# A two-dimensional scan block on one core: the order of small matmuls, copies and stores between the stages of a pair

## The chip, the core and the metric

The kernel runs on one core of one Trainium2 chip, as one program. The metric is the device time of the whole program in microseconds. The engines that matter are TensorE (PE, matmuls; PEld, its weight loads), VectorE (DVE), ScalarE (ACT), GpSimd (POOL) and SyncE (SP), which issues the DMAs. All data are fp32. An fp32 matmul shows in the trace as two records, called passes here.

## What is computed

The input x has the shape (4, 128, 96, 96). It is group-normalised, read as four sequences of 9216 positions (row by row, column by column, and both backwards), and each sequence runs through the same block. The reference, cut to what matters:

```python
t = _grouped1x1(x, in_proj_w, in_proj_b, G)          # 4 groups of 32 channels -> 512
u, gate = t[:, :HID], t[:, HID:]                     # HID = 256
u = depthwise_conv5(silu(u), dw_w)
s = ssm_in_w @ u                                     # 32 channels
a = clip(DMIN + (DMAX - DMIN) * sigmoid(ssm_delta_w @ u + ssm_delta_b), 1e-4, 0.9999)
bb, cc = tanh(ssm_b_w @ u + ssm_b_b), tanh(ssm_c_w @ u + ssm_c_b)
hst = scan(h = a * h + bb * s)                       # along the sequence
u = u + ssm_out_w @ (cc * hst + ssm_d * s)
y = out_proj_w @ (mix(u * sigmoid(gate)) + mix_b) + out_proj_b
```

The four outputs are put back in image order, concatenated, multiplied by fuse_w (128 x 512) and added to x. Before the loop the kernel folds mix, out_proj and fuse of each direction into one weight `w_fin`, called W below.

## The kernel before

**Tiling.** An image is done in two phases, V (columns) and H (rows). A phase has NS = 6 steps, a step 4 x 384 positions. The positions of a step are dealt to R = 4 residues p, so that an instruction works on 384 columns. A unit is one residue of one direction. A *pair* is the units of both directions (s = 0 and 1), and `pair(t)` (L747) runs 192 times; t counts pairs, i = 2t is the pair's first unit, k = t % 4 its residue, and bi = i - 12 is the unit that is finished in this pair (LAG = 6 pairs behind). There is a prologue before the first pair and a `tail` for the last six.

**What a pair does,** in the order in which it is written out by hand (there is a manual schedule, so every engine takes its instructions in this order):

- `front` (L413): only in the steps of the first half of a phase. It computes silu(in_proj) of a later step, 32 small matmul records in 32x32 tiles, and four Silu on ScalarE (L476). The second half of a phase goes backwards over the same data, so it loads what `keep_silu` (L449) stored to DRAM. `load_front` (L249) loads x_in.
- `taps` (L599): the conv of channels 128 to 255, one tap on ScalarE (L609), four on VectorE (L611), summed in PSUM banks 0 and 1, the last one written to u.
- `conv` (L576): the conv of channels 0 to 127 on TensorE, matmuls with 128 rows and the weight `band`; `conv_less` (L585) adds the taps that need only 64 rows, with the weight `less`, and copies both banks to u.
- `accumulate` (L700): W for a unit finished earlier, eight matmuls with 32 columns each, a copy `ys` on ScalarE (L712, L714), and an addition to the image in SBUF on GpSimd (L728).
- `under` (L498): ScalarE seeds the PSUM banks of ssm_out with u (L501), s = 1 in banks 2 and 3, s = 0 in banks 0 and 1.
- `gates_and_out` (L536): four matmuls for the gate (L487), 32 rows and 128 columns, and four for ssm_out (L493) of the same form; then `sigmoids` (L503), four Tanh on ScalarE (L509). A gate is needed in both halves of a phase. In the second half it comes from DRAM (`load_kept`, L522), or from the buffer, and the pair is *old*.
- `gating` (L552): VectorE multiplies u by the gate (L563).
- `proj` (L623): the four projections of u, in PSUM banks 4 and 5 (`PROJ`), first all of channels 128 to 255 (j = 1), then of 0 to 127 (j = 0); Tanh, copy and Tanh on ScalarE (L639 to L641); the decay (L644) and a product (L647) on GpSimd.
- `scale_s` (L662): ScalarE multiplies s by ssm_d (L664). `scan` (L670) is on VectorE, `outputs` (L685) on GpSimd.

**Kinds of pairs,** from the seventh pair on. From `fresh` (L245) and `mirror` (L259), with t % 24: 8 to 17 have gates and no front (gates alone, 80 of the 192); 20 to 23 and 0 to 5 have old gates and a front; 18 and 19 old gates and no front; 6 and 7 gates and a front. Where there is no front, `plan` (L124) gives banks 7 and 6 to the conv and banks 4 and 5 to W; with a front it is the other way round. In the pairs without a front the order on TensorE is: band, W, W, less, gates and ssm_out, projections. There the banks of the gates are banks 4 and 5 (after both W) and 7 and 6 (after the copies of u).

**Queues.** [...] `later` holds pieces of the next image's statistics, done in pairs with k > 1 (`stats_piece`, L782), where VectorE also reads chunks of the next image (L397).

Of the kernel before, what the change touches and what calls it, by code (L numbers as in the profile page):

```python
# [55 lines left out]
R = 4  # L56
# [10 lines left out]
def conv_preact_kernel(  # L67
# [53 lines left out]
    FRONT = (7, 6, 2, 3)  # L121
    GATE = {True: (6, 4, 5, 7), False: (4, 5, 7, 6)}

# [293 lines left out]
    def front_parts(i, banks):  # L417

        step, g = divmod(i, R)
        if step * UB >= NU:  # L420
            return
        st = step % NS
        if st == NS // 2:
            sils[step] = sils[step - 1]
            load_silu(step + 1, (g,))
        elif st == NS - 1 and g < 2:
            load_silu(step, (2 * g, 2 * g + 1))
        elif g == 0 and fresh(step):
            sils[step] = wk.tile([P, 2, 2, 4, N + 1], F32, tag="sil", name=f"sil_{step}")
        if fresh(step):  # L430
            yield from compute_front(step, g, banks)
        sil = sils[step]

        if st == 0:
            engine = nc.gpsimd if step else nc.vector
            for s in range(2):
                engine.memset(sil[64 * s : 64 * s + 64, s, 0, g, 0:1], 0.0)
            if g < 2:
                engine.memset(sil[:, :, 1, g, 0:1], 0.0)

        for s in range(2):
            load_front(step + 1, s, slice(64 * s + 32, 64 * s + 64), slice(g, g + 1))
        if g == R - 1:
            for s in range(2):
                load_front(step + 1, s, slice(64 * s, 64 * s + 32), slice(0, R))
        if step:
            keep_silu(step, g)

    def keep_silu(step, g):  # L449
        st = step % NS  # L450
        if st < NS // 2 - 1:
            nc.sync.dma_start(kept_sil[step // NS % 2][st][g], sils[step][:, :, :, g, :])

# [48 lines left out]

    def sigmoids(bi, banks):  # L503
        bn = stats[units[bi]["b"]][1]
        n = bi // 2
        gv = gates[n % 2]
        for s in range(2):
            for j in range(2):
                nc.scalar.activation(  # L509
                    gv[:, s, j, :],  # L510
                    bank(banks[2 * s + j])[:, :N],
                    AF.Tanh,
                    bias=bn[:, 2 + j : 3 + j],
                    scale=0.5,
                )
# [20 lines left out]
    def gates_and_out(bi, with_front):  # L536
# [4 lines left out]
        if with_front:  # L541
            gate(bi, 1, 0, to[2])
        out_of(bi, 1, 0)
        out_of(bi, 0, 0)
        out_of(bi, 0, 1)
        out_of(bi, 1, 1)
        if not with_front:
            gate(bi, 1, 0, to[2])
        gate(bi, 1, 1, to[3])
        sigmoids(bi, to)  # L550
# [25 lines left out]
    def conv(i, banks):  # L576

        step, p = units[i]["step"], units[i]["p"]
        sil, k = blocks(step), less_of(p)
        for s in range(2):  # L580
            for g in range(4):
                mm(bank(banks[s]), g, band[:, s, p, g, :], columns(step, sil[s][:, g, :], 1 - k),
                   True, False)

    def conv_less(i, banks, copies=(nc.scalar.copy, nc.scalar.copy)):  # L585
        step, p = units[i]["step"], units[i]["p"]
        sil, k = blocks(step), less_of(p)
        for g in range(4):
            for s in range(2):
                r = less_rows(s, p)  # L590
                mm(bank(banks[s]), g, less[r, p, g, :], columns(step, sil[s][r, g, :], k),
                   False, True)
        for s, copy in enumerate(copies):
            copy(us[i][:, s, 0, :], bank(banks[s])[:, :N])  # L594

# [26 lines left out]

    def proj(i, banks):  # L623

# [6 lines left out]

        for j in (1, 0):
            for bk, cols in zip(banks, ((qb, qb, qa, qa), (qs, qs, qc, qc))):
                for c in range(4):
                    mm(bank(bk), c, w_proj[:, j, cols[c]], us[i][:, c % 2, j, :], j == 1, j == 0)
        pa, pb = (bank(bk)[:, :N] for bk in banks)
# [98 lines left out]

    later = []

# [9 lines left out]
    def pair(t):  # L747
# [10 lines left out]
        if back:  # L758
            front(t + R, FRONT)
        if seed and not with_front:  # L760
            under(bi, 1)
# [30 lines left out]
        if waiting and not late:  # L792
            accumulate(waiting.pop(0), w[0])()
        if seed and not with_front:
            under(bi, 0)
        if ahead:
            accumulate(waiting.pop(0), w[1])()
            free[0] = w[0]
            stats_piece()

            other = nc.vector.tensor_copy if k > 1 and not old else nc.scalar.copy
            conv_less(i, banks, (nc.scalar.copy, other))
        if old:
            for s in range(2):
                for j in range(2):
# [11 lines left out]
        if back:  # L817
            load_kept(bi // 2 + 2)
            if waiting:
# [3 lines left out]
            first_tap(i + 2)  # L823
            scale_s(i - 2)
        if t == NU // 2 - 1:
            for s in range(2):
                under(bi + 2, s)
        proj(i, PROJ)
        if not back and t > 0:
            scale_s(i - 2)  # L830
# [5 lines left out]
        if t == NU // 2 - 3:  # L836
            load_last()
        if t < R:
            keep_silu(0, t)

# [137 lines left out]
```

## Time and profile before

| | |
|---|---|
| time, median of 3 runs | 1869.76 us (1868.79 to 1873.79) |
| profiled run, span | 1866.4 us, granted TensorE clock 0.990 |
| TensorE busy | 1827.3 us (98%) |
| VectorE busy | 1561.9 us (84%) |
| ScalarE busy | 1542.6 us (83%) |
| GpSimd busy | 1567.0 us (84%) |
| DMA | 321.21 MB, mean 172 GB/s |

Of the profile four things are read. The busy shares say which engine has no time left. The chain of waits follows the last instruction back to whatever released it. The groups give the mean duration of each form of instruction and the idle time before it. The timeline shows the instructions in order, merged where one engine repeats the same one, with the idle time before each and what ended it. The start of the projections, which every pair has once, is a good mark: from one to the next is the length of a pair. A busy TensorE is not TensorE at its peak: passes that overlap show as longer records, so the distance between the starts of passes is what counts.

### The profile page before, as it was taken

Reading aid. Unit: us, or ns where it says so; the run is one execution under the profiler, and the core shown is the slowest. Engines: PE = TensorE matmul, PEld = TensorE weight load, DVE = VectorE, ACT = ScalarE, POOL = GpSimd, SP = SyncE. Lnnn points to the kernel's source line nnn. Section 1 sums busy time; section 2 is a strip of 40 time slices with the busy share of each in tenths; the row PEclk is TensorE's granted clock in tenths of the full one; section 3 lists DMA queues with packets and bytes.
Section 4 is the critical chain, followed back from the end, with each engine's and each line's share of the span. In section 5 each row is a group of like instructions: output and inputs, shape, how many; then the busy total and the mean of one; then the engine's idle time right before and its main releaser. Section 6 shows DMA issues by size and latency. Waiting matters only on the chain.

```text
span 1866.4 us, 57669 instructions
## 1 busy us (share of the span) xinstructions
PE 1827.3 (98%) x24024; PEld 691.4 (37%) x24024; DVE 1561.9 (84%) x1573; ACT 1542.6 (83%) x2841; POOL 1567.0 (84%) x1615
## 2 busy tenths in 40 slices
PE   6899999999999999999999999999999999999998
PEld 3234333443334433344333433334333443334432
DVE  4698878888888988888889898888887888878886
ACT  4688888888888888888888888888888888888875
POOL 6388988888879899888887989888888889997886
PEclk7999999999999999999999999999999999999999
DMA  5564463433875557243596556433467634535424
GB/s 194 162 197 145 146 207 118 168 141 126 274 244 202 169 155 215 86 158 131 186 301 217 167 162 207 152 130 126 139 224 234 231 113 156 191 118 175 145 102 171
DMA packets 147828, 321.21 MB, mean 172 GB/s; under 512 B 14192, under 2 KB 115696, under 8 KB 147568
## 3 DMA queue, kind: packets, MB, share of 16 engines
q1 hardware_dynamic: 147136, 316.56, 51.5%
q8 instruction: 190, 3.11, 0.7%
q10 hardware_dynamic: 432, 0.96, 0.1%
q14 instruction: 70, 0.57, 0.1%
HBM read 185.21 MB, written 132.25 MB: 170 GB/s over the span
## 4 chain that ended last, share of the span: by engine, by line
PE 87%; ACT 4%; POOL 3%; DVE 2%; DMA 1%; issue 1%; SPq 0%; POOLq 0%; DVEq 0%; ACTq 0%
PE psum L133 73%; PE psum L487 7%; PE psum L493 7%; ACT sil L476 1%; DMA xs<-in_xr 1%; ACT psum L609 1%; DVE u L563 1%; DVE psum L611 1%; POOL acc L728 1%; POOL t L644 1%; ACT u L594 0%; POOL t L647 0%; DMA x_in<-in_xs 0%; POOL t L687 0%; POOL t L688 0%
## 5 line engine op out<-in xcount | busy, mean ns | idle before, releaser
L611 DVE SCALAR_TENSOR_TENSOR psum<-sil,small,psum 128x768 f32<-128x768 f32 x576 | 589.0, 1023 | 39.1 <-ACT psum L609 13.5
L133 PE MATMUL psum<-u,w_fin 128*32 128x384 f32 x6144 | 535.6, 488 | 0.0
L133 PE MATMUL psum<-u,main 128*32 128x384 f32 x6144 | 534.9, 489 | 0.3 <-DVE u L611 0.3
L563 DVE SCALAR_TENSOR_TENSOR u<-gate,psum 128x768 f32<-128x768 f32 x376 | 349.9, 952 | 165.9 <-ACT u L594 91.6
L728 POOL TENSOR_TENSOR acc<-ys,acc 128x384 f32<-128x384 f32 x376 | 412.7, 1118 | 21.6 <-ACT ys L714 4.3
L687 POOL TENSOR_TENSOR t<-t,t 64x384 f32<-64x384 f32 x192 | 263.8, 1374 | 78.0 <-DVE t L681 58.0
L133 PEld LDWEIGHTS psum<-u,w_fin 128*32 128x32 f32 x6144 | 195.9, 110 | 303.3 <-issue 223.6
L501 ACT COPY psum<-u 128x768 f32<-128x768 f32 x352 | 277.6, 802 | 34.9 <-DVE u L611 28.8
L133 PE MATMUL psum<-sil,band 128*32 128x384 f32 x3072 | 291.9, 494 | 10.8 <-ACT tm L639 8.2
L133 PEld LDWEIGHTS psum<-u,main 128*32 128x32 f32 x6144 | 181.8, 109 | 324.9 <-issue 203.0
L644 POOL TENSOR_SCALAR t<-tm 64x384 f32<-64x384 f32 x191 | 177.9, 931 | 133.0 <-ACT tm L639 103.2
L688 POOL TENSOR_TENSOR t<-t,t 64x384 f32<-64x384 f32 x192 | 276.3, 1439 | 15.1
L609 ACT ACTIVATE psum<-sil,small 128x768 f32<-128x768 f32 x192 | 174.1, 907 | 104.6 <-DVE u L563 98.6
L493 PE MATMUL psum<-t,main 32*128 32x384 f32 x1536 | 240.2, 520 | 3.3 <-POOL t L688 1.5
L647 POOL TENSOR_TENSOR t<-t,tm 64x384 f32<-64x384 f32 x192 | 208.9, 1088 | 15.3
L509 ACT ACTIVATE gate<-psum,bnorm 128x384 f32<-128x384 f32 x384 | 194.8, 583 | 13.9 <-PE psum L487 7.7
L476 ACT ACTIVATE sil<-psum,bnorm 128x385 f32<-128x385 f32 x384 | 192.0, 585 | 11.7 <-DMA xs<-in_xr 5.4
L611 DVE SCALAR_TENSOR_TENSOR u<-sil,small,psum 128x768 f32<-128x768 f32 x192 | 194.9, 1015 | 7.8
L487 PE MATMUL psum<-x_in,wn 32*128 32x384 f32 x768 | 193.8, 521 | 0.5 <-ACT u L594 0.3
L594 ACT COPY u<-psum 128x384 f32<-128x384 f32 x352 | 153.1, 482 | 30.1 <-PE psum L133 21.8
L714 ACT COPY ys<-psum 128x384 f32<-128x384 f32 x287 | 132.5, 475 | 49.5 <-PE psum L133 41.5
L133 PE MATMUL psum<-sil,less 64*32 64x384 f32 x3072 | 168.8, 497 | 0.0
(87 smaller groups left out, 1642.0 us busy)
## 6 DMA issues: line engine op xcount, KB each, us to landing
sil<-sil SPq DMA_DIRECT2D x128, 770.0 KB, 6.2
kept<-gate SPq DMA_DIRECT2D x80, 768.0 KB, 3.9
gate<-kept SPq DMA_DIRECT2D x76, 768.0 KB, 5.0
x_in<-in_xs SPq DMA_DIRECT2D x192, 96.2 KB, 2.5
out<-acc SPq DMA_DIRECT2D x48, 384.0 KB, 6.1
acc<-in_xr SPq DMA_DIRECT2D x38, 384.0 KB, 6.3
xs<-in_xr SPq DMA_DIRECT2D x72, 192.0 KB, 5.1
x_in<-in_xs SPq DMA_DIRECT2D x184, 48.1 KB, 4.7
```

Source lines behind the costliest of these rows:

```text
L133: nc.tensor.matmul(o[r, : rhs.shape[-1]], lhsT, rhs, start=start, stop=stop, skip_group_check=True)
L476: nc.scalar.activation(sil[:, s, j, g, :], bank(banks[2 * s + j])[:, : N + 1], AF.Silu, bias=bn[:, 1:2] if j else bn[:, 4 + g : 5 + g],)
L487: nc.tensor.matmul(bank(to)[:, :N], stats[un["b"]][0][r, s, :], x_in[s][r, q, off : off + N], start=True, stop=True)
L493: nc.tensor.matmul(bank(SSM + 2 * s + j)[:, :N], w_so[r, bass.ts(j, P)], z[r, :], start=bi not in seeded, stop=True, skip_group_check=True)
L501: nc.scalar.copy(psum[:, SSM + 2 * s : SSM + 2 * s + 2, :N], us[bi][:, s])
L563: nc.vector.scalar_tensor_tensor(v, g, 1.0, pz, ALU.add, ALU.mult)
L611: nc.vector.scalar_tensor_tensor(us[i][:, :, 1, :] if k == K - 1 else part, src, w_tap[:, k : k + 1], part, ALU.mult, ALU.add,)
L644: nc.gpsimd.tensor_scalar(*op)
L647: nc.gpsimd.tensor_mul(ta[0:64, p, :], tb[0:64, :], tm[0:64, :])
L687: nc.gpsimd.tensor_mul(ta[0:64, p, :], tb[64:P, :], ta[64:P, p, :])
L688: nc.gpsimd.tensor_add(tb[0:64, :], ta[0:64, p, :], tb[0:64, :])
L728: adder.tensor_add(part, y, part)
```

## The change

It reorders work in the pairs without a front, and moves some DMAs.

- In gates-alone pairs (`between`), `less` and its copy of u come between the first and the second W. Until now it came after both.
- Where the conv is in banks 6 and 7, the copy of u is one instruction over both banks on ScalarE; it was two of 384 columns, the second on VectorE where k > 1. The conv's two banks change places.
- The banks of the gates in those pairs are 4, 7, 6, 5 in place of 4, 5, 7, 6; the third Tanh is that of bank 5. Ssm_out of s = 0, whose seed is written late, comes last among the four, and the third gate is put between.
- In gates-alone pairs the projections are done bank by bank: all of bank 4, then all of bank 5, with j = 0 first.
- `scale_s` is done after the projections in pairs that compute gates, and ahead of ssm_out in old pairs; it was ahead of the projections in both.
- The stores of silu go through a list, `to_keep`. In the first four pairs 1, 2, 1 and 0 of them are issued, and from the third step on one with each front. Afterwards the order is as it was.
- `load_kept` of a pair with k = 2 is issued in the next pair, behind the loads of its front (`soon`).

```diff
-    GATE = {True: (6, 4, 5, 7), False: (4, 5, 7, 6)}
+    GATE = {True: (6, 4, 5, 7), False: (4, 7, 6, 5)}
@@ front_parts, keep_silu
-        if step:
-            keep_silu(step, g)
+        if st < NS // 2 - 1:
+            to_keep.append((step, g))
+        if step > 1:
+            keep_silu(1)
@@ sigmoids
-            for j in range(2):
+            for j in (0, 1) if s == 0 or to[0] == GATE[True][0] else (1, 0):
@@ gates_and_out, without a front
-        out_of(bi, 1, 0)
-        out_of(bi, 0, 0)
-        out_of(bi, 0, 1)
-        out_of(bi, 1, 1)
-            gate(bi, 1, 0, to[2])
-        gate(bi, 1, 1, to[3])
+            out_of(bi, 1, 0)
+            gate(bi, 1, 0, to[2])
+            out_of(bi, 1, 1)
+            out_of(bi, 0, 1)
+            out_of(bi, 0, 0)
+            gate(bi, 1, 1, to[3])
@@ conv_less
-        for s, copy in enumerate(copies):
-            copy(us[i][:, s, 0, :], bank(banks[s])[:, :N])
+        if banks == PROJ:
+            for s in range(2):
+                nc.scalar.copy(us[i][:, s, 0, :], bank(b0 + s)[:, :N])
+        else:
+            nc.scalar.copy(us[i][:, :, 0, :], psum[:, b0 : b0 + 2, :N])
@@ proj
-        for j in (1, 0):
-            for bk, cols in zip(banks, ((qb, qb, qa, qa), (qs, qs, qc, qc))):
-                for c in range(4):
-                    mm(bank(bk), c, w_proj[:, j, cols[c]], us[i][:, c % 2, j, :], j == 1, j == 0)
+        turns = [(e, j) for j in (1, 0) for e in range(2)]
+        for e, j in sorted(turns) if apart else turns:
+            for c, cols in enumerate(((qb, qb, qa, qa), (qs, qs, qc, qc))[e]):
+                first, end = (j == 0, j == 1) if apart else (j == 1, j == 0)
+                mm(bank(banks[e]), c, w_proj[:, j, cols], us[i][:, c % 2, j, :], first, end)
@@ pair
+        for n in soon:
+            load_kept(n)
+        soon.clear()
...
+        between = ahead and not old
+        if between:
+            conv_less(i, banks)
         if seed and not with_front:
             under(bi, 0)
         if ahead:
             accumulate(waiting.pop(0), w[1])()
             free[0] = w[0]
+            if not between:
+                conv_less(i, banks)
             stats_piece()
-            other = nc.vector.tensor_copy if k > 1 and not old else nc.scalar.copy
-            conv_less(i, banks, (nc.scalar.copy, other))
         if old:
+            scale_s(i - 2)
...
-            load_kept(bi // 2 + 2)
+            if k == 2 and t + 1 < NU // 2:
+                soon.append(bi // 2 + 2)
+            else:
+                load_kept(bi // 2 + 2)
...
-            scale_s(i - 2)
...
-        proj(i, PROJ)
-        if not back and t > 0:
+        proj(i, PROJ, between)
+        if not old and t > 0:
             scale_s(i - 2)
...
-        if t < R:
-            keep_silu(0, t)
+        keep_silu((1, 2, 1, 0)[t] if t < R else 0)
```

## The prediction

> **What bounds the kernel now.** I read the page first: engine shares, then the chain that ended last.
>
> ```profile
> PE 1827.3 (98%) x24024; PEld 691.4 (37%) x24024; DVE 1561.9 (84%) x1573; ACT 1542.6 (83%) x2841; POOL 1567.0 (84%) x1615
> ...
> PE 87%; ACT 4%; POOL 3%; DVE 2%; DMA 1%; issue 1%; SPq 0%; POOLq 0%; DVEq 0%; ACTq 0%
> ```
>
> TensorE carries the span, so only three things can move the time: fewer passes, cheaper joints between stages, and waits at the head of TensorE's queue. The change removes no matmul. I therefore cut the timeline of TensorE at every start of the projections (psum<-u,main), which gives one length per pair. A typical gates-alone pair, from the timeline of all engines (start us, length us, engine, line, operation, in brackets the idle time before it):
>
> ```profile
> 379.72 2.79 PE L133 MATMUL psum<-u,main 128*32 128x384 f32 x32
> ...
> 382.32 1.47 PE L133 MATMUL psum<-sil,band 128*32 128x384 f32 x16
> ...
> 383.62 2.76 PE L133 MATMUL psum<-u,w_fin 128*32 128x384 f32 x32
> ...
> 386.00 0.80 ACT L501 COPY psum<-u 128x768 f32<-128x768 f32 x1 [0.20 <-DVE u L611]
> 386.31 0.88 PE L133 MATMUL psum<-sil,less 64*32 64x384 f32 x16
> 386.73 0.47 ACT L714 COPY ys<-psum 128x384 f32<-128x384 f32 x1
> 387.12 0.73 PE L487 MATMUL psum<-x_in,wn 32*128 32x384 f32 x2
> ...
> 387.27 0.86 ACT L594 COPY u<-psum 128x384 f32<-128x384 f32 x2
> ...
> 388.19 0.58 PE L487 MATMUL psum<-x_in,wn 32*128 32x384 f32 x1
> ...
> 389.03 1.18 PE L133 MATMUL psum<-u,main 128*32 128x384 f32 x12
> ```
>
> The pair is 389.03 - 379.72 = 9.31 us. Projections, band and W run without a hole (2.60, 1.30, 2.69; eight passes of 0.32 are 2.58). The gate stage does not: four rounds of passes, 1.28 us of work, last from 387.12 to 389.03, 1.91 us. The last gate starts at 388.19, 0.06 us after the second copy of u ends (387.27 + 0.86 = 388.13), and the next projections follow 0.84 us later. So this wait sets the pair.
>
> In the 32 pairs with k > 1 the second copy of u is on VectorE, and there it comes late behind batch statistics:
>
> ```profile
> 621.25 1.02 DVE L397 BATCH_NORM_STATS2 bn<-xs 128x6 f32<-128x384 f32 x2
> ...
> 622.18 0.54 DVE L594 COPY u<-psum 128x384 f32<-128x384 f32 x1
> 622.23 1.46 PE L487 MATMUL psum<-x_in,wn 32*128 32x384 f32 x3
> ...
> 623.62 1.82 PE L133 MATMUL psum<-u,main 128*32 128x384 f32 x20
> ```
>
> Gates began at 621.00, so this stage took 2.62 us. Over all 80 gates-alone pairs the cut gives a mean of 9.43 us (most of those with k < 2 at 9.30, the best with k = 3 at 9.05). The others are full: pairs with old gates and a front stand at 9.26, old gates without a front at 8.25, with no hole in TensorE. Two holes outside are large, one at the start and one at 255 us:
>
> ```profile
> 63.81 1.25 SPq L452 DMA_DIRECT2D sil<-sil  x2
> ...
> 74.75 2.00 ACT L476 ACTIVATE sil<-psum,bnorm 128x385 f32<-128x385 f32 x4 [5.36 <-DMA xs<-in_xr]
> ...
> 77.27 2.79 PE L133 MATMUL psum<-sil,band 128*32 128x384 f32 x16 [5.18 <-ACT tm L639]
> ...
> 255.52 0.88 PE L133 MATMUL psum<-x_in,wn 32*32 32x385 f32 x16 [0.87 <-DMA x_in<-in_xs]
> ```
>
> At 74.75 ScalarE wants to write the third step's silu into the buffer of the first, whose store to DRAM was issued at 63.81 (the row names another DMA of the same queue; the store is what the buffer needs). The pair lasts 13.41 us, where its neighbours last about 7. At 255 us the front waits for x_in; that pair lasts 12.96 instead of 9.26.
>
> **What the Trainium skill says.** "TensorEngine Tiling (Array Packing)", Key Properties: changing the tiling mode drains TensorE. The trace agrees: W to W has no joint, W to less costs 2.69 - 2.58 = 0.11 us, and less takes 0.81 us for two passes of 0.32. "TensorE: Matmul & The Clock Gate", The mechanism: a weight load overlaps running matmuls only if its row group differs. That fits a gate that arrives late: its two passes lie 0.43 us apart instead of 0.32. "ScalarE: Activation LUTs", Rules for kernel authors: about 0.83 ns an element. The copies here agree: 128x384 takes 482 ns and 128x768 802 ns, (802 - 482)/384 = 0.83, which leaves 0.16 us for each instruction. "DMA: Bandwidth & Descriptors", Issuing engines are not separate DMA queues: all transfers share the same 16 engines. The trace around 250 us, with these engines almost full, agrees.
>
> **The change, part by part, in a gates-alone pair (80 of 192).** Less between both W costs one joint more. W1 to less is 1.29 + 0.11 = 1.40, less to W2 0.81, W2 to gates 1.43. The last two are seen in pairs with gates and a front:
>
> ```profile
> 98.00 0.88 PE L133 MATMUL psum<-sil,less 64*32 64x384 f32 x16
> 98.81 1.50 PE L133 MATMUL psum<-u,w_fin 128*32 128x384 f32 x16
> ...
> 100.23 0.60 PE L487 MATMUL psum<-x_in,wn 32*128 32x384 f32 x3
> ```
>
> The stretch grows from 2.69 + 0.81 = 3.50 to 3.64, so +0.14 us. In return the copy of u starts one W earlier. With G the start of the gates, less starts at G - 2.24. ScalarE begins a copy 0.96 after less starts (387.27 - 386.31), so at G - 1.28. One copy of 128x768 takes 0.80 (L501's duration; the new form goes from PSUM to SBUF and isn't shown, two copies at 0.86 are the other bound) and ends at G - 0.48. ScalarE's queue then holds the seed of s=0 (0.80, until G + 0.32) and the second ys (0.47, until G + 0.80). The gates into banks 4, 7 and 6 and all ssm_out find their banks ready. Only the last gate, now in bank 5, waits for that ys: it starts at G + 0.86 instead of G + 1.07, and the projections follow 0.84 later. The stage is 1.70 instead of 1.91, the pair 2.60 + 1.29 + 3.64 + 1.70 = 9.23 where it was 9.30. If successive ScalarE copies overlap as two L501 in a row do (1.54 for two), it is 9.19. I take 9.20. The floor, with no wait in the gates, is 4 x 0.32 plus the joint of 0.21 (ssm_out alone: 0.86 for two passes), 1.49, so a pair of 9.02.
>
> The larger part is the outliers: no copy is left on VectorE, so the 0.3 to 0.7 us behind statistics and clips vanish. 80 x (9.43 - 9.20) = 18 us. Not all goes: three pairs carry an extra W (1.29 us each), three wait for the statistics' small matmul (0.7 us each, now directly ahead of a gate in the same bank), and the first pair after the gates-with-front pairs starts late. I leave 6 us of excess there, and count 12 us.
>
> The remaining edits here hide. Bank-by-bank projections release bank 4 1.3 us earlier, and the tanh on it waits behind the first tap anyway (ends 2.02 after the projections start). Bank 5 needs its tanh-gate at +1.3, and this comes third of four, done at about +0.8. Ssm_out of s=0 last delays VectorE's gating nothing, since that waits for the second gate's tanh at G + 1.95, and the last ssm_out ends at about G + 1.55. Scale_s behind the projections moves 0.6 us out of the time before the next tanh; queued after it are the seed and ys, and ScalarE has about 0.7 us of idle time there. In old pairs scale_s fits in the 1.07 us in which ScalarE waits for VectorE's gating. ScalarE's sum is about 8.5 us of 9.2, VectorE's and GpSimd's at most 8.6.
>
> Stores of silu at the start: after three pairs four are issued where eight were nearly all out, and the first step's last store goes a pair earlier. ScalarE's 5.4 us should vanish and the band behind it run normally: 13.41 to about 7, -6 us. The load of kept gates behind x_in, where k = 2: of the 3.7 us at 255 I take 3.5. Elsewhere it hides under full TensorE.
>
> Sum: 12 + 6 + 3.5 = 21.5; 1869.8 - 21.5 = 1848.
>
> **Rivals.** (a) The waits in the gates vanish fully, 9.02 a pair: another 80 x 0.18 = 14 us, 1834. Against it: seed and ys stand between u and the last gate on ScalarE. (b) ScalarE becomes the limit: the first tap, now later, pushes tanh, seed and ys, and the gate stage keeps 1.91. Then the pair is 9.44, the outliers' gain is eaten, and the DMA part alone remains: 1860. The 8.5 of 9.2 us speaks for it, the idle 0.68 us before the first ys against it. (c) Slower: later ys and larger copies make VectorE's taps late, and the seed waits for them; 0.3 us more than 9.43 in 80 pairs is +24 us, and if the loads only move the stall elsewhere, nothing comes off: 1890. Against it, VectorE has more room after the change, because it loses a copy of 0.55 us.
>
> **How the numbers follow.** My forecast 0.62, (a) 0.14, (b) 0.16, (c) 0.08. The forecast and (a) are faster by over 0.3% (below 1864). (b) lies close to that edge, so I split it, 0.06 faster and 0.10 same. That makes faster 0.82, same 0.10, slower 0.08. The range reaches from (a), 1834, to (b) with half of the DMA part missing, 1866. It leaves out (c), the rest of (b) and what lies below (a).
>
> **What would show it.** Right: most gates-alone pairs 9.15 to 9.25, no copy of u on VectorE in the groups; the copy of u a single 128x768 of about 800 ns; the gate stage about 1.7, its last gate started by ys; no wait over 3 us at 70 and 255 us; old-gate pairs unchanged at 9.26 and 8.25. Wrong: W1-less-W2 longer than 3.7, a last gate released later than G + 0.9, a seed that waits for VectorE, or new holes where the loads now meet.

## Result, and the profile after

| | before | after |
|---|---|---|
| time, median | 1870.35 us (1868.79 to 1873.79, 4 runs) | 1842.08 us (1841.98 to 1843.84, 4 runs) |
| ratio, 95% interval | | 0.9849 [0.9832, 0.9866] |
| profiled span | 1866.4 us | 1840.3 us |

The time fell by 28 us where 21.5 were forecast; 1842 us lies between the ends of the forecast, 1834 and 1866. The page of the kernel after, busy shares and the chain that ended last (its line numbers are up to 18 higher than those of before for the same code):

```profile
PE 1806.1 (98%) x24024; PEld 650.3 (35%) x24024; DVE 1544.8 (84%) x1541; ACT 1569.2 (85%) x2773; POOL 1564.1 (85%) x1615
...
PE 94%; ACT 3%; POOL 1%; DVE 1%; issue 0%; DVEq 0%; POOLq 0%; ACTq 0%
```

TensorE still has the same 24024 matmul records and is as full as before. What changed is the chain: TensorE's own share of it rose from 87% to 94%, ScalarE's fell from 4% to 3% and GpSimd's from 3% to 1%. So the kernel got faster because waits at the head of TensorE's queue went, not because work went. The 32 instructions that VectorE has less are copies of u, as the groups by form show (line, engine, operation, output<-input with its shape, count, then busy us, mean ns, idle time before with its releaser):

```profile
L608 ACT COPY u<-psum 128x768 f32<-128x768 f32 x100 | 80.0, 800 | 20.2 <-PE psum L133 20.0
L606 ACT COPY u<-psum 128x384 f32<-128x384 f32 x184 | 79.3, 484 | 25.1 <-PE psum L133 24.6
```

No row of a VectorE copy of u is left, and the new form, which the trace of before did not have, takes 800 ns.

An ordinary gates-alone pair, from the timeline of all engines (start us, length us, engine, line, operation):

```profile
363.86 2.79 PE L133 MATMUL psum<-u,main 128*32 128x384 f32 x32
...
366.46 1.47 PE L133 MATMUL psum<-sil,band 128*32 128x384 f32 x16
...
367.76 1.47 PE L133 MATMUL psum<-u,w_fin 128*32 128x384 f32 x16
...
369.16 0.88 PE L133 MATMUL psum<-sil,less 64*32 64x384 f32 x16
...
369.96 1.50 PE L133 MATMUL psum<-u,w_fin 128*32 128x384 f32 x16
370.14 0.80 ACT L608 COPY u<-psum 128x768 f32<-128x768 f32 x1 [0.20 <-PE psum L133]
370.84 0.81 ACT L505 COPY psum<-u 128x768 f32<-128x768 f32 x1
371.39 0.59 PE L491 MATMUL psum<-x_in,wn 32*128 32x384 f32 x2
...
371.58 0.48 ACT L729 COPY ys<-psum 128x384 f32<-128x384 f32 x1
...
372.15 0.55 PE L491 MATMUL psum<-x_in,wn 32*128 32x384 f32 x1
...
372.34 1.05 ACT L514 ACTIVATE gate<-psum,bnorm 128x384 f32<-128x384 f32 x2 [0.27 <-PE psum L491]
...
372.97 0.14 PEld L133 LDWEIGHTS psum<-u,main 128*32 128x32 f32 x5 [0.56 <-ACT gate L514]
372.97 0.53 PE L133 MATMUL psum<-u,main 128*32 128x384 f32 x4
```

The copy of u now runs under the second W: it starts at 370.14 and is done 0.45 us before the gates begin at 371.39. Behind it ScalarE has the seed and the second ys, which ends at 371.58 + 0.48 = 372.06. The last gate starts 0.09 us after that, at 372.15, and the projections 0.82 later.

The projections, however, do not start because that gate is done. They write bank 4 first, and the first Tanh of the gates has to read bank 4 before. It starts at 372.34 and takes 0.58 us, to 372.92; the weights of the projections are loaded 0.05 us later, and their row (PEld) names it. In the kernel before that Tanh (388.06 to about 388.64) was done 0.38 us before the weights of the projections (389.02), so there the late gate did count. Three pairs of the kernel after tell the two apart. They hold the statistics' small matmul, which delays the gates, so that ys is long done. This is pair 38:

```profile
380.69 0.48 ACT L729 COPY ys<-psum 128x384 f32<-128x384 f32 x1
...
381.61 0.59 PE L491 MATMUL psum<-x_in,wn 32*128 32x384 f32 x2 [0.36 <-DVE bnorm L238]
...
382.55 1.05 ACT L514 ACTIVATE gate<-psum,bnorm 128x384 f32<-128x384 f32 x2 [1.38 <-PE psum L491]
...
383.18 0.16 PEld L133 LDWEIGHTS psum<-u,main 128*32 128x32 f32 x8 [0.62 <-ACT gate L514]
```

Here ys ends at 381.17, 0.44 us before the gates begin, and from the gates to the projections it is 383.18 - 381.61 = 1.57 us, as in the ordinary pair (1.58). So ys holds the last gate there but costs nothing. It has little room: in pair 61 it ends 0.28 us later, and the stage is 1.84.

The stages, each from one start on TensorE to the next:

| us | projections | band | W, less, W | gates and ssm_out | pair |
|---|---|---|---|---|---|
| before | 2.60 | 1.29 | W, W, less: 2.69 + 0.81 = 3.50 | 1.91 | 9.30 |
| forecast | 2.60 | 1.29 | 3.64 | 1.70 | 9.20 (sum 9.23) |
| after | 2.60 | 1.30 | 1.40 + 0.80 + 1.43 = 3.63 | 1.58 | 9.11 |

At the start of the program, the place of the 5.36 us wait:

```profile
69.12 2.01 ACT L480 ACTIVATE sil<-psum,bnorm 128x385 f32<-128x385 f32 x4
...
71.65 0.85 PE L133 MATMUL psum<-sil,band 128*32 128x384 f32 x8 [0.16 <-ACT tm L654]
```

Neither line has a long wait before it any more. In the pair that took 12.96 us before (pair 24, which now begins at 240.76) the wait for x_in is gone too: the 32 small matmuls of the front follow the projections at once.

```profile
240.76 2.79 PE L133 MATMUL psum<-u,main 128*32 128x384 f32 x32
243.47 1.01 PE L133 MATMUL psum<-x_in,wn 32*32 32x385 f32 x32
244.41 1.50 PE L133 MATMUL psum<-sil,band 128*32 128x384 f32 x16
```

A part of what these two places cost before was no wait. In the trace of before the granted clock of TensorE is 0.50 from 75.48 to 82.31 us and from 256.39 to 259.80, and the band there takes 2.79 us for 16 records in place of 1.47. In the trace of after the clock is 1.00 from 40.17 to 1811.69. In the gates-alone pairs it is 1.00 in both, so the clock has no part in their gain.

TensorE's timeline cut at every start of the projections, and the pairs added up by kind (pair t reaches from the start of the projections of t - 1 to its own):

| pairs | before, us | after, us | difference |
|---|---|---|---|
| up to the first projections | 40.1 | 41.0 | +0.9 (40.1 to 41.3 over all runs) |
| pairs 1 to 5 | 42.6 | 34.2 | -8.4 |
| gates alone, 80 | 754.8 | 739.8 | -15.0 |
| old gates and a front, 70 | 659.4 | 653.1 | -6.3 |
| old gates, no front, 20 | 165.9 | 166.9 | +1.0 |
| gates and a front, 16 | 163.7 | 165.4 | +1.7 |
| after the last projections | 39.9 | 39.9 | 0 |

The sum is -26.1 us, the difference of the two spans. The gain sits in the gates-alone pairs and in five pairs at the start. Of the 6.3 us in the pairs with old gates and a front, 3.6 are pair 24. Two rows of pairs got worse, which the forecast did not have. The first old pair behind gates-alone pairs takes 8.41 us instead of 8.25, eight times: VectorE's last tap ends 0.32 us later there, the seed waits for it, and ssm_out begins 0.16 us later. The other row is taken up below.

### The profile page after: what moved, and what is told of

It reads as the page before. It is cut to its first block, busy times and chain, and to the rows that moved or that the text cites. A ratio compares the mean times of both kernels' runs of the same rounds, so it can differ in the third digit from the quotient of the medians.

```text
span 1840.3 us, 57440 instructions
## 1 busy us (share of the span) xinstructions
PE 1806.1 (98%) x24024; PEld 650.3 (35%) x24024; DVE 1544.8 (84%) x1541; ACT 1569.2 (85%) x2773; POOL 1564.1 (85%) x1615
## 4 chain that ended last, share of the span: by engine, by line
PE 94%; ACT 3%; POOL 1%; DVE 1%; issue 0%; DVEq 0%; POOLq 0%; ACTq 0%
PE psum L133 80%; PE psum L497 8%; PE psum L491 5%; ACT sil L480 1%; ACT psum L623 0%; ACT u L606 0%; ACT t L656 0%; ACT t L679 0%; ACT tm L654 0%; ACT t L655 0%; DVE psum L625 0%; DVE u L574 0%; POOL t L702 0%; POOL t L703 0%; POOL band L343 0%
## 5 line engine op out<-in xcount | busy, mean ns | idle before, releaser
L133 PE MATMUL psum<-u,w_fin 128*32 128x384 f32 x6144 | 552.2, 489 | 0.0
L133 PEld LDWEIGHTS psum<-u,w_fin 128*32 128x32 f32 x6144 | 188.0, 110 | 321.0 <-issue 219.8
L662 POOL TENSOR_TENSOR t<-t,tm 64x384 f32<-64x384 f32 x192 | 201.7, 1050 | 15.3
L491 PE MATMUL psum<-x_in,wn 32*128 32x384 f32 x768 | 162.3, 528 | 2.4 <-ACT u L606 1.3
L133 PEld LDWEIGHTS psum<-sil,band 128*32 128x32 f32 x3072 | 89.2, 109 | 183.8 <-issue 89.7
```

The source lines that it names most:

```text
L133: nc.tensor.matmul(o[r, : rhs.shape[-1]], lhsT, rhs, start=start, stop=stop, skip_group_check=True)
L491: nc.tensor.matmul(bank(to)[:, :N], stats[un["b"]][0][r, s, :], x_in[s][r, q, off : off + N], start=True, stop=True)
L662: nc.gpsimd.tensor_mul(ta[0:64, p, :], tb[0:64, :], tm[0:64, :])
```

## Experiments

The theory: two independent parts, the order of stores at the start, and a shorter wait in the gates of 80 pairs, which by the forecast ends with ys. Rivals: the loads only move a stall, ScalarE becomes the limit, or one of the small edits does the work alone. Each run has its own runs of the kernel before on the same chip, and its ratio is against these.

**The DMA edits alone.** The kernel before, with its compute order untouched:

```diff
-        if step:
-            keep_silu(step, g)
+        if st < NS // 2 - 1:
+            to_keep.append((step, g))
+        if step > 1:
+            keep_silu(1)
...
-            load_kept(bi // 2 + 2)
+            if k == 2 and t + 1 < NU // 2:
+                soon.append(bi // 2 + 2)
+            else:
+                load_kept(bi // 2 + 2)
```

> The kernel before, with only the two edits of the DMAs: the list of stores of silu, and the later load of kept gates where k = 2. My theory (the stores hold up ScalarE at 70 us, the load holds up x_in at 255 us, both apart from the gates): about 1870 - 8 - 3.6 = 1858 us, ratio 0.994; the pair at 69 us falls from 13.4 to about 6.6 us, the one at 251 us from 13.0 to about 9.3, gates-alone pairs keep their mean of 9.43. Rival (the stall only moves to a later pair, and the gain after the change comes from the gates alone): 1868 to 1872 us, and a new pair of over 12 us.

Measured: 1859.65 us (1856.6 to 1864.9), ratio 0.9949 [0.9933, 0.9965], 10.8 below before, and 6.5 to 12.5 by the interval. Pairs 1 to 5 take 34.1 us, all of the gain that they have in the kernel after; the gates-alone pairs keep their median of 9.30. So the two parts are separate. The sign that the rival named, a new pair of over 12 us, appears all the same: pair 104 takes 13.44 us instead of 10.80. A gate waits 1.37 us for ys there, and the granted clock is 0.50 for the next 3.4 us. The mean of the gates-alone pairs is 9.49 for that reason, not 9.43. Which of the two edits makes the gain is asked below.

**The stores alone, undone.** The kernel after, with the stores at the start issued when they were before:

```diff
-        if step > 1:
-            keep_silu(1)
+        if step:
+            kept_now(step, g)          # issues the store of this step and residue at once
...
-        keep_silu((1, 2, 1, 0)[t] if t < R else 0)
+        if t < R:
+            kept_now(0, t)
```

> The kernel after, with the stores of silu in the old order at the start (two in each of the first four pairs). Theory: ScalarE waits again for the store of the first step's last part before it writes the third step's silu, the pair at about 69 us lasts 13.4 instead of 6.5 us: 1842 + 7 = 1849 us. Rival (the wait was for x_in or for the chunks of the next image, which the row of the profile names): 1842 to 1844 us.

Measured: 1850.71 us, ratio 0.9906 [0.9891, 0.992]. The kernel after, run again beside it, took 1842.60 us (1841.55 to 1842.82), ratio 0.9863 [0.9846, 0.9879]. The stores are worth 8.1 us. The old wait is back, in the timeline of this kernel:

```profile
64.20 1.25 SPq L455 DMA_DIRECT2D sil<-sil  x2
...
75.54 2.00 ACT L485 ACTIVATE sil<-psum,bnorm 128x385 f32<-128x385 f32 x4 [4.38 <-DMA xs<-in_xr]
...
78.06 2.79 PE L133 MATMUL psum<-sil,band 128*32 128x384 f32 x16 [3.57 <-ACT tm L659]
```

The row names the load of xs, and yet only the order of stores was changed. The landings of the DMAs in the trace settle it. The second of the two stores, that of the first step's last part, is issued at 64.83 and lands at 75.36, 0.18 us before ScalarE begins; the loads of xs issued behind it land only at 75.84 and 76.33. In the kernel before that store lands at 74.56, 0.19 us before ScalarE's 74.75. In the kernel after it lands at 63.57, long before it is needed at 69.12. So it was right to distrust the name.

The half clock comes back as well: 0.50 from 69.70 to 73.12 us and from 76.53 to 83.36. The three traces with the old order of stores (before, one copy alone, this one) have such stretches at the start, and the ten others have none between 42 us and 1000.

**The load of the kept gates, undone.** The kernel after, where the load is issued in its own pair again:

```diff
-            if k == 2 and t + 1 < NU // 2:
-                soon.append(bi // 2 + 2)
-            else:
-                load_kept(bi // 2 + 2)
+            load_kept(bi // 2 + 2)
```

> The kernel after, with the load of kept gates where k = 2 back in its own pair, ahead of the next front's x_in. Theory (the load took the DMA engines from x_in): the pair of 251 us shows a wait for x_in again, 3 us or more, about 1845.5 us. Rival (where such a wait falls depends on how the transfers of a run happen to meet, and the order of issue settles nothing): within 1 us of the kernel after, 1841 to 1843.5 us, no wait over 1 us there or one elsewhere.

Measured: 1842.39 us, ratio 0.9863 [0.9848, 0.9878], against 1842.60 for the kernel after on that chip. No difference shows. In its trace pair 24, the one with 12.96 us before, takes 10.89 and pair 28 10.39, while pair 25, which takes 9.87 in the kernel after, takes 9.27. The 70 pairs together differ by 1.9 us from those of after, in a profile of the slowest of its four runs (1844.11).

The other traces say more of pair 24. In all ten kernels with the later load it takes 9.33 us; in the three without it takes 12.96, 9.98 (one copy alone) and 10.89. So the wait in this pair does go with the edit. But part of it comes back elsewhere: pair 25 takes 9.26 to 9.69 without the edit and 9.27 to 10.46 with it. The DMA engines are full there: in the trace of before they are busy all of the time from 245 to 250 us. In the time of the whole kernel the forecast gain of 3.5 us is not shown.

**One copy of u alone.** The kernel before with one ScalarE copy of both banks, and the conv in ascending banks that this needs, but less still after both W:

```diff
+        ... b0 = min(banks)
...
-        for s, copy in enumerate(copies):
-            copy(us[i][:, s, 0, :], bank(banks[s])[:, :N])
+        if banks == PROJ:
+            for s in range(2):
+                nc.scalar.copy(us[i][:, s, 0, :], bank(b0 + s)[:, :N])
+        else:
+            nc.scalar.copy(us[i][:, :, 0, :], psum[:, b0 : b0 + 2, :N])
```

> The kernel before, with only the copy of u made one ScalarE instruction of 128x768 (and with the conv's two banks in ascending order, which it needs); less stays behind both W. My theory: the last two gates wait for the end of this copy, about G + 0.95, so the stage is about 1.85 and the pair 9.24 for every k; 80 x (9.43 - 9.24) = 15 us less, minus 4 us of excess that has other causes: about 1859 us, ratio 0.994. Rival (the gain in the gates comes from the place of less and not from the copy's engine): gates-alone pairs stay at 9.3 to 9.4 on average, 1866 to 1872 us. A second rival (one copy is all that counts and the place of less is idle): pairs at 9.11, 1846 us.

Measured: 1866.3 us (12 runs), ratio 0.9977 [0.9967, 0.9987]. The ordinary gates-alone pairs take 9.27 whatever k is, so the outliers of k > 1 go with the VectorE copy, as forecast. But only 4 of the expected 11 us come. Pairs 56, 104 and 152, which hold an extra W, take 12.87, 12.38 and 11.34 where they had 10.78, 10.80 and 10.73, and that eats 4.3 of the 5.0 us that the other 77 gates-alone pairs win. Only 0.7 us of the gain is theirs; 3.0 are pair 24 in this trace. Pair 56 of this kernel:

```profile
557.76 1.50 PE L133 MATMUL psum<-sil,band 128*32 128x384 f32 x16 [0.60 <-ACT ys L717]
...
560.06 3.81 POOL L731 TENSOR_TENSOR acc<-ys,acc 128x384 f32<-128x384 f32 x2 [0.77 <-DMA acc<-in_xr]
...
564.43 0.58 PE L487 MATMUL psum<-x_in,wn 32*128 32x384 f32 x1 [0.95 <-ACT ys L717]
```

Two things meet here. The band, now in ascending banks, begins in bank 6, which the ys of the extra W has yet to empty. And GpSimd waits for the load of an image, then ys for GpSimd's addition, and at last a gate for ys. The first comes with the edit. The second depends on when a load lands, which the three different lengths agree with. Pair 24 has 9.98 us here, although no DMA edit is in this kernel: the stall of 12.96 is not a fixed one either.

**Less after both W.** The kernel after, with only the place of the small conv matmuls undone:

```diff
-        between = ahead and not old
-        if between:
-            conv_less(i, banks)
...
-            if not between:
-                conv_less(i, banks)
+            conv_less(i, banks)
```

> The kernel after, with less and the copy of u behind both W again, everything else left. My theory (the new order of gates needs an early copy): the copy ends about G + 0.95, and the second gate of the queue, in bank 7, waits for it and holds everything behind it; the stage becomes 0.95 + 0.06 + 0.43 + 0.32 + 0.32 + 0.42 = 2.5 us, the pair 9.9, 80 x 0.8 = 64 us more than the kernel after: about 1905 us, slower than before. Rival (the place of less hardly matters, the gain is from one copy and the banks): 1840 to 1850 us.

Measured: 1905.31 us, ratio 1.0191 [1.0174, 1.0208]: slower than before. Its pairs take 9.92 instead of 9.11, and 80 x 0.81 = 65 us is about the whole difference of 63 us to the kernel after. Its timeline at the gates:

```profile
364.91 1.61 PE L491 MATMUL psum<-x_in,wn 32*128 32x384 f32 x3
365.09 0.80 ACT L608 COPY u<-psum 128x768 f32<-128x768 f32 x1
...
365.94 0.59 PE L497 MATMUL psum<-t,main 32*128 32x384 f32 x1
...
367.43 1.50 PE L133 MATMUL psum<-u,main 128*32 128x384 f32 x16
```

Now the second gate of the new order, in bank 7, waits until the copy of both banks ends at 365.89; the gate stage lasts 367.43 - 364.91 = 2.52 us. The new gate order is good only with the copy a W earlier.

**The old gate order.** The kernel after with the banks and the order of gates and ssm_out of before:

```diff
-    GATE = {True: (6, 4, 5, 7), False: (4, 7, 6, 5)}
+    GATE = {True: (6, 4, 5, 7), False: (4, 5, 7, 6)}
...
-            for j in (0, 1) if s == 0 or to[0] == GATE[True][0] else (1, 0):
+            for j in range(2):
...
             out_of(bi, 1, 0)
-            gate(bi, 1, 0, to[2])
-            out_of(bi, 1, 1)
-            out_of(bi, 0, 1)
             out_of(bi, 0, 0)
+            out_of(bi, 0, 1)
+            out_of(bi, 1, 1)
+            gate(bi, 1, 0, to[2])
             gate(bi, 1, 1, to[3])
```

> The kernel after, with the old banks (4, 5, 7, 6) and the old order of gates and ssm_out in the pairs without a front, and the old order of tanh. Theory (what counts is that the gate behind the second W stands last in TensorE's queue): the second gate waits for the second ys, G + 0.73, and holds the queue; stage 0.73 + 0.43 + 0.32 + 0.32 + 0.42 = 2.2, pair 9.75, 1842 + 51 = 1893 us. Rival (the early copy alone makes the gain): 9.11 to 9.3, 1842 to 1857 us.

Measured: 1891.26 us, ratio 1.0106 [1.0091, 1.0121], with pairs of 9.75 us. The reason is on the same rows:

```profile
342.65 1.31 PE L491 MATMUL psum<-x_in,wn 32*128 32x384 f32 x3
342.84 0.48 ACT L729 COPY ys<-psum 128x384 f32<-128x384 f32 x1
...
344.87 1.50 PE L133 MATMUL psum<-u,main 128*32 128x384 f32 x16
```

The gate second in the queue goes to bank 5, which ys frees only at 343.32; six instructions wait behind it. In the kernel after the same ys holds back the last gate alone, where it costs nothing.

**The projections together.** The kernel after with the old order inside `proj`:

```diff
-        proj(i, PROJ, between)
+        proj(i, PROJ)
```

> The kernel after, with the projections in the old order (both banks with j = 1, then both with j = 0) in gates-alone pairs. The prediction called the bank-by-bank order hidden. Theory (hidden): gates-alone pairs stay at 9.11, 1842 us. Rival, from the timeline of the kernel after: bank 5 is now read by the third of the four tanh of the gates, which ends about G + 2.5, while the old order writes bank 5 at 0.65 us after the projections start, G + 2.23; TensorE waits about 0.33 us in every pair, 9.44, and the kernel takes 1842 + 26 = 1868 us.

Measured: 1862.32 us, ratio 0.9951 [0.9934, 0.9968], 20 us more than after. The theory that this edit is hidden falls; the rival's pair of 9.44 was near the measured 9.41. The whole difference is inside the projections:

```profile
338.89 3.08 PE L133 MATMUL psum<-u,main 128*32 128x384 f32 x32
...
341.79 1.47 PE L133 MATMUL psum<-sil,band 128*32 128x384 f32 x16
```

They last 2.90 instead of 2.60 us. The old order wants bank 5 after two passes, at 0.67 us. In this trace the third Tanh, which empties bank 5, ends 0.89 us after the projections start, and the third round of passes starts at 0.94 instead of 0.67. Bank by bank asks for bank 5 at 1.3. That the Tanh is what it waits for follows from these times; the row itself names no releaser.

**A copy on VectorE.** The kernel after, with the second half of u copied by VectorE in pairs with k > 1:

```diff
-        if banks == PROJ:
+        if banks == PROJ or apart:
             for s in range(2):
-                nc.scalar.copy(us[i][:, s, 0, :], bank(b0 + s)[:, :N])
+                copy = nc.vector.tensor_copy if apart and s else nc.scalar.copy
+                copy(us[i][:, s, 0, :], bank(b0 + s)[:, :N])
...
-            conv_less(i, banks)
+            conv_less(i, banks, k > 1)
```

> The kernel after, with the copy of u in two halves where k > 1 in gates-alone pairs, the second on VectorE as before. It waits in VectorE's queue behind the last tap, the clip and the statistics, and a gate in bank 6 or 7 waits for it in the middle of the queue. My theory (the outliers come from this copy): pairs with k < 2 stay at 9.11, those with k > 1 go to 9.5 to 10.0; 32 x 0.6 = 19 us more: about 1860 us. Rival (the copy, now a W earlier, is early enough on any engine): 1842 us, all pairs 9.11.

Measured: 1870.21 us (12 runs), ratio 1.0001 [0.9992, 1.001]. Pairs with k < 2 stay at 9.11; those with k > 1 take 9.36 to 10.89. The copy stands behind the statistics in VectorE's queue, and the second gate behind the copy:

```profile
588.46 0.54 DVE L397 BATCH_NORM_STATS2 bn<-xs 128x6 f32<-128x384 f32 x1
588.92 0.54 DVE L607 COPY u<-psum 128x384 f32<-128x384 f32 x1
...
589.51 0.58 PE L491 MATMUL psum<-x_in,wn 32*128 32x384 f32 x1 [0.87 <-DVE u L607]
```

The direction was expected, the size was not: 28 us in place of about 18. Behind the statistics in VectorE's queue, this one copy costs as much as the whole change gains.

**Scale_s ahead of the projections.** The kernel after loses time in a few pairs, and two edits came into question: the ascending conv banks, and scale_s, which now stands behind the projections. A losing pair in the kernel after, one with an extra W:

```profile
543.00 1.47 PE L133 MATMUL psum<-u,w_fin 128*32 128x384 f32 x16
...
544.35 0.61 ACT L679 ACTIVATE t<-t,small 64x384 f32<-64x384 f32 x1
544.99 0.48 ACT L729 COPY ys<-psum 128x384 f32<-128x384 f32 x1
...
545.52 1.50 PE L133 MATMUL psum<-sil,band 128*32 128x384 f32 x16 [1.05 <-ACT ys L729]
```

The band waits 1.05 us for a ys, and scale_s (L679) runs just ahead of it. So scale_s went back:

```diff
+        if back and not old:
+            scale_s(i - 2)
         proj(i, PROJ, between)
-        if not old and t > 0:
+        if not back and t > 0:
             scale_s(i - 2)
```

> The kernel after, with scale_s ahead of the projections again in the pairs that compute gates. Theory (its new place buys nothing in gates-alone pairs, since ScalarE has idle time on either side, and it costs in the pairs with gates and a front and behind the extra W): gates-alone pairs 9.11, the three pairs of 10.18 back to 9.68, the three of 11.63 to about 11.0; 1842 - 3.4 = 1838.5 us. Rival (the earlier tanh of the projections matters, because W waits for bank 4 and GpSimd starts later): gates-alone pairs 9.2 or more, over 1848 us.

Measured: 1842.45 us, ratio 0.9847 [0.9832, 0.9862], no gain. Pairs 55, 103 and 151, with gates and a front, go back to their 9.68, as expected. But pairs 25, 73, 121 and 169, which this edit does not touch itself, take 10.44 to 10.54 instead of 9.8 to 9.9, where the second half of the front waits for VectorE. What was won was lost there. How the one brings about the other is open.

**Three repairs together.** The kernel after, where the conv begins with bank 7 if there is no front, scale_s stands ahead of the projections only in pairs with gates and a front and behind the extra W elsewhere, and the small matmul of the statistics comes between less and the second W:

```diff
-        for s in range(2):
+        for s in range(2) if banks == PROJ else (1, 0):      # in conv
...
         if between:
             conv_less(i, banks)
+            free[0] = w[0]
+            stats_piece()
...
+        first = back and not old and with_front
+        if first:
+            scale_s(i - 2)
         proj(i, PROJ, between)
```

> The kernel after, with three repairs where the profile shows losses: the conv without a front starts with bank 7 (the copy of the extra W's bank 6 then hides behind half of band); scale_s stays ahead of the projections in pairs with gates and a front, and stands behind the extra W elsewhere; the piece of the statistics is between less and the second W, not ahead of the gates. Theory (the losses are these waits): the three pairs of 11.63 fall to about 10.5, the three of 10.18 to 9.68, the three of 10.22 to about 9.6, gates-alone pairs stay at 9.11: 1842 - 3.4 - 1.5 - 1.9 = 1835 us. Rival (these waits only uncover others behind them, such as GpSimd's additions): 1840 to 1842 us.

Measured: 1839.12 us (1838.85 to 1840.42), ratio 0.9831 [0.9816, 0.9845], the fastest kernel here. The kernel with scale_s alone put back, on the same chip, took 1841.83 to 1843.15. The band behind an extra W waits no more:

```profile
541.42 1.47 PE L133 MATMUL psum<-u,w_fin 128*32 128x384 f32 x16
...
542.71 1.64 PE L133 MATMUL psum<-sil,band 128*32 128x384 f32 x16
...
542.96 0.48 ACT L729 COPY ys<-psum 128x384 f32<-128x384 f32 x1
```

The pairs with the statistics' matmul fall from 10.22 to 9.81, pairs 55, 103 and 151 to 9.68, and pairs 56 and 152 from 11.63 to 10.63 and 10.54. Pair 104 takes 12.01, by the chain from GpSimd over ys to a gate again (the DMA in the first row is again only the name that the row gives):

```profile
991.92 3.82 POOL L743 TENSOR_TENSOR acc<-ys,acc 128x384 f32<-128x384 f32 x2 [0.47 <-DMA x_in<-in_xs]
...
995.77 0.48 ACT L729 COPY ys<-psum 128x384 f32<-128x384 f32 x1 [0.72 <-POOL acc L743]
...
996.30 0.91 PE L491 MATMUL psum<-x_in,wn 32*128 32x384 f32 x2 [0.28 <-ACT ys L729]
```

Pairs 73 and 169 again take 10.5. That is about 3 us less than the kernel after takes (1842.08, on another chip), where 7 were expected: part of the repair comes back as waits in other pairs.

## Why the prediction was right, point by point

**W, less, W.** Forecast 3.64 us, measured 3.63. Pricing each joint from another kind of pair that already had it worked.

**The gate stage** was mis-sized, 1.70 us forecast and 1.58 measured, and its last wait is another one. Up to ys the working holds. Less starts at G - 2.23 (forecast -2.24) and the copy at G - 1.25 (-1.28), with the forecast 0.80 us. The three instructions on ScalarE start 0.70 and 0.74 us after one another, and the last lasts 0.48: 1.92 us for copy, seed and ys in place of 0.80 + 0.80 + 0.47 = 2.07. So ys ends at G + 0.67 instead of G + 0.80 and the last gate starts at G + 0.76 instead of G + 0.86. The prediction named this overlap and counted one of the two (its own numbers then give 9.17, not 9.19). What it left out is bank 4. The first gate is done at G + 0.91, its Tanh runs from G + 0.94 to G + 1.53, and the projections start at G + 1.58, also where ys ends 0.44 us before G. The floor of 1.49 counted TensorE's passes alone; with the Tanh it is 1.58, and the kernel after stands on it. That the Tanh is this last wait is read from the trace; no run here moves it.

**The outliers** were not the larger part of the gain, as the prediction calls them. By its own numbers the ordinary pair was to give 80 x 0.10 = 8 us and the outliers about 4 of the 12. Measured, the ordinary pair gives 80 x 0.19 = 15 us. The excess of the other pairs over the ordinary one is 10.8 us before and 11.0 after. The copy on VectorE is gone, and putting it back brings late pairs with k > 1 back. But 3 x (11.63 - 9.11) = 7.6 us are now in the pairs with an extra W and 3 x (10.22 - 9.11) = 3.3 in those with the statistics' matmul. The sum was to be 80 x 9.20 + 6 = 742 us and is 739.8. That it comes so close is in part luck, since too small a gain in the ordinary pair and too large a one in the outliers cancel.

**The edits that hide.** This step failed in part. Bank-by-bank projections cost nothing, as the prediction said, but the reason was half told: without them the new tanh order costs 0.30 us a pair. And two edits have a price that was set at nothing. The ascending conv banks with scale_s before ys cost 3 x 0.85 us in the pairs with an extra W, and scale_s behind the projections costs 3 x 0.5 us in pairs 55, 103 and 151, where it pushes the four Silu of the front back. These are rare kinds of pairs, whose own timeline the prediction had not read for these edits; it checked scale_s against the idle time of an ordinary pair. A gain was missed as well: in the pairs with old gates less now stands ahead of the statistics' matmul, and hides its wait. The timeline of before, and then that of after:

```profile
287.13 2.76 PE L133 MATMUL psum<-u,w_fin 128*32 128x384 f32 x32
290.34 0.38 PE L186 MATMUL psum<-mv,gmean 128*128 128x1 f32 x2 [0.45 <-ACT ys L714]
290.66 0.88 PE L133 MATMUL psum<-sil,less 64*32 64x384 f32 x16
```

```profile
274.12 2.76 PE L133 MATMUL psum<-u,w_fin 128*32 128x384 f32 x32
276.81 0.88 PE L133 MATMUL psum<-sil,less 64*32 64x384 f32 x16
277.62 0.38 PE L186 MATMUL psum<-mv,gmean 128*128 128x1 f32 x2
```

The 0.45 us wait is gone, 0.5 us in each of three pairs.

**The stores at the start.** Right in mechanism, 6 us forecast, 8.1 measured: pair 5 went from 13.41 to 6.51 and not only to 7, and pair 4 from 8.37 to 7.17, since its front had waited too. The store's landing shows the wait that was named. Up to 2.5 us of the gain are the half clock (an estimate: half of the 5.04 us for which TensorE is busy in that stretch of before), which the pair of 13.41 holds without the prediction's naming it.

**The load of the kept gates.** The 3.5 us are not shown. Pair 24 does fall by 3.6 us between the two profiles, but that this fits the forecast is luck. The profile of before shows two waits for x_in there, 0.25 and 0.87 us, and then the half clock for 3.41 us, which can account for up to 1.7 us (an estimate: half of it). Without the edit the pair has taken 9.98 and 10.89 us too, and undoing the edit costs nothing that can be measured in the whole kernel. The stall of one profile was taken for a fixed cost.

**The rivals.** Rival (a), waits in the gates that vanish fully, is in substance what came; its 9.02 a pair was too low by the 0.09 us that the Tanh adds, and 9.11 lies halfway between it and the forecast. Rival (b), ScalarE as the limit that keeps the stage at 1.91, falls: the stage is 1.58, and ScalarE is idle for 0.27 us just before the first Tanh. Rival (c), taps of VectorE so late that seeds wait, falls as a whole. The seeds' waits for taps add up to 9.1 us of ScalarE's idle time, against 28.8 before. Only in the eight first old pairs does it cost something, 1.3 us together.

In all: about 8 us from the stores, 15 from the gates-alone pairs, and in the profiles 3.6 from pair 24 and 1.5 from the three pairs above; the runs do not pin the rest to one edit. The total of 21.5 was too low because the ordinary pair and the stores gave more than forecast, while one of its three parts, the load, is not shown at all.

## What to carry to other kernels

When one engine is full, look for the wait at the head of its queue and order that queue by when each operand comes free; in two of these kernels one ys holds back seven instructions or only one, by nothing but the order of the gates and ssm_out, and holding back the one costs nothing. To know whether a wait still counts, look for pairs in which it is absent: here three pairs without it are no shorter in that stage. A floor is more than the passes of the full engine; it has to hold the detour over another engine that frees the next bank. A reordering is worth something only with those that fit it: with less moved back, or the old gate order, or the old projections, the same kernel takes 63, 49 and 20 us more. Before an edit is costed at nothing, look at the rare kinds of pairs as well as the ordinary one, and don't book the removal of a DMA stall that one profile shows until a second trace has it in the same place.

## What was not expected of the hardware

- Instructions that follow one another on ScalarE start before the one ahead has ended by the record: 0.70 us after the start of a copy of 0.80, 0.74 after one of 0.81. Over the three instructions behind the last gate that makes 0.15 us.
- One copy of 128x768 from PSUM to SBUF takes 800 ns, two of 128x384 together 0.86 us, so joining them saves only 0.06; its use is in going early, and in being off VectorE.
- The releaser that a row names can be another DMA of the same queue: the 4.38 us "<-DMA xs<-in_xr" comes and goes with the order of the stores alone, and ScalarE begins 0.18 us after the store's landing and before that of the xs load issued next.
- The granted clock of TensorE was 0.50 for 6.8 us beginning within a hole of 5.18 us (before), and for 3.4 us behind one of 0.87 us (before) and one of 1.37 us (the DMA edits alone). Behind the hole of 1.05 us at 545 us of the kernel after it stayed at 1.00. So a hole can cost more than its own length, and its length alone does not say when.
